# A graph-attention layer by leading columns: a new order of the drain, and tiles that start on round addresses

## The chip, the cores and the metric

The kernel runs on one core of a Trainium2 chip. The metric is device time in microseconds (us) of one execution; before the change it is 244.22 us, the median of 15 executions (243.28 to 246.55). Engines: TensorE (PE, with its weight loads PEld), VectorE (DVE), ScalarE (ACT), GpSimd (POOL) and SyncE (SP), which only issues transfers. Every engine works through its own queue in order; a wait at the head of a queue holds up all that stands behind it.

## The reference

`N = 4096` rows, `D = 512` features, 4 heads, all in float32:

```python
ht = (h @ W).reshape(N, N_HEADS, N_HIDDEN).transpose(1, 0, 2)
src = einsum('hnd,hd->hn', ht, a[:, :N_HIDDEN, 0])
dst = einsum('hnd,hd->hn', ht, a[:, N_HIDDEN:, 0])
e = leaky_relu(src[:, :, None] + dst[:, None, :], 0.01) + adj_mat[None]
att = softmax(e, axis=-1)
g = einsum('hij,hjd->hid', att, ht).mean(axis=0)
out = layernorm(x + g)          # over the 512 features, eps 1e-5
```

The adjacency matrix (4096 x 4096, 64 MB) holds values up to 1e9 that are added to the scores. Where the largest entry of a row lies far enough above the second, softmax puts all weight on that one column, and the row's result is `x[column] @ mean of the heads of W`.

## The kernel before, in words

`leading_rows` computes all rows in that way and tests that it was allowed; `general`, behind a branch, recomputes blocks in which a row failed the test. With these inputs no block is recomputed.

Rows are cut into 32 blocks (NB) of 128. With Q = 4, LATE = 28 and BEHIND = 24. Iteration `t` of the main loop works on several blocks at once:

- SP loads the adjacency rows of block t + 5 (`load_adj`, L113; 2 MB, 16 KB in each of 128 partitions; blocks 0 and 28 to 31 in four pieces of 4 KB per partition). Six buffers `adj_t` hold them. x comes into the big tile `hold` in groups of four blocks (`load_x`, L116); W lies in the places of blocks 16 to 31 of `hold` at first, so the x of blocks 24 to 31 is loaded only after the loop.
- VectorE takes the maxima of 64 segments of each row of block t (`segment_maxima`, L158), finds the leading segment (`find_segment`, L165 to L167), and GpSimd gathers that segment (`lead`, L171) by an indirect DMA.
- For block t - 2 VectorE finds the column within the segment (`find_column`, L193), GpSimd adds (L195) and gathers the rows of x (`y`, L181). Block 31 is searched in its whole row instead (`find_column_in_row`, L201, 4096 columns).
- For block t - 3 TensorE transposes y in four pieces (`turn`, L208), ScalarE copies the result to SBUF (`yt`, L210), and TensorE multiplies by the mean of the heads in four products over a quarter of the features each (`products`, L221). Blocks below BEHIND get x added on TensorE by a product with the identity (`residual`, L214).
- ScalarE does the layer norm's statistics with accumulating passes (`stats`, L243 and L245), the sum of squares of x for the test (`row_norm`, L228) and the final scaling (`finish`, L261); GpSimd makes the reciprocal root (`rstd`, L248 to L250). The results of blocks 24 to 27 are copied out of PSUM (`put_by`, L234) into a free adjacency buffer.

The order of every queue is the order of the program text. After the loop comes the drain, also written out by hand. It holds the loads of x for blocks 24 to 31, the 18 stores (L306, all on SP, each waiting for its data in the order of the program), the last two searches, the products of blocks 29 to 31, the addition of x to blocks 24 to 27 on VectorE (`add_x`, L237), the test in three parts (`bound`, L360 to L370, `test`, L376 to L382, `count`, L386, `report`, L390 to L393), and the normalisation: blocks 24 to 27 by `stats`, `rstd` or `rstd_late` (L254 to L257) and `finish`; blocks 28, 29 and 30 by `finish_last` (L294 to L303: add x, statistics and scaling on VectorE, only the root on ScalarE); block 31, whose products are in two halves of 256 columns (`products_of_half`, L270), by `finish_in_halves` (L279 to L286).

Where the tiles start, in bytes within a partition: `hold` at 17,312 (160 past a multiple of 256), the first `adj_t` at 96,992 (224 past one; all six alike), the first `y` at 204,032 (a multiple of 256), the first `lead` at 196,896 (32 past one). Tiles of the pools lie one behind the other, each rounded up to 32 bytes.

Of the kernel before, what the change touches and what calls it, by code (L numbers as in the profile page):

```python
# [9 lines left out]
F32 = mybir.dt.float32  # L10
# [3 lines left out]
OP = mybir.AluOpType  # L14
# [3 lines left out]
EPS = 1e-5  # L18
# [48 lines left out]
def leading_rows(ctx, tc, x, adj, W, a, out, ident, v, n_bad, any_bad):  # L67
# [17 lines left out]

    once = ctx.enter_context(tc.tile_pool(name="once", bufs=1))
    adj_pool = ctx.enter_context(tc.tile_pool(name="adj_pool", bufs=AHEAD + 1))
    small = ctx.enter_context(tc.tile_pool(name="small", bufs=5))
    rows = ctx.enter_context(tc.tile_pool(name="rows", bufs=2))
    psum = ctx.enter_context(tc.tile_pool(name="psum", bufs=4, space=bass.MemoryType.PSUM))  # L90
# [4 lines left out]
    out_rows = out.rearrange("(p nb) d -> p nb d", nb=NB)  # L95
    w_blocks = W.rearrange("(kb p) (h d) -> p kb h d", p=P, h=H)

    hold = once.tile([P, NB, D], F32, name="hold")
    w_at = NB - KB * H
    w_sum = once.tile([P, KB, D], F32, name="w_sum")  # L100
    a_rows = once.tile([2 * H, D], F32, name="a_rows")

    adj_t = {}

    def pieces(ib):
# [9 lines left out]
    def load_x(lo, n):  # L115
        nc.sync.dma_start(hold[:, ds(lo, n), :], x_rows[:, ds(lo, n), :])  # L116
# [46 lines left out]
    def find_segment(ib):  # L163
        seg = seg_of.pop(ib)
        nc.vector.max(out=top[:, ib, :], in_=seg)  # L165
        at = small.tile([P, 8], U32, name="at")
        nc.vector.max_index(at, top[:, ib, :], seg)  # L167
        row = small.tile([P, 1], U32, name="row")
        nc.gpsimd.tensor_tensor(row, at[:, 0:1], first[:, ib : ib + 1], op=OP.add)  # L169
        lead = small.tile([P, E], F32, name="lead", bufs=2 * Q + 1)  # L170
        nc.gpsimd.indirect_dma_start(  # L171
            out=lead, out_offset=None, in_=adj_segs,
            in_offset=bass.IndirectOffsetOnAxis(ap=row[:, :1], axis=0),
        )
        start = at_of[ib] = small.tile([P, 1], U32, name="start")
        nc.gpsimd.tensor_tensor(start, at[:, 0:1], width, op=OP.mult)
        lead_of[ib] = lead

    def gather_rows(ib, col):
        y = y_t[ib] = rows.tile([P, D], F32, name="y", bufs=4)  # L180
        nc.gpsimd.indirect_dma_start(  # L181
            out=y, out_offset=None, in_=x,
            in_offset=bass.IndirectOffsetOnAxis(ap=col[:, :1], axis=0),
        )

    def find_inner(ib):
        nc.vector.max(out=inner[:, ib, :], in_=lead_of[ib])

    def find_column(ib):
        if ib < BEHIND:  # L190
            find_inner(ib)
        within = small.tile([P, 8], U32, name="within")
        nc.vector.max_index(within, top[:, ib, :], lead_of[ib])  # L193
        col = small.tile([P, 1], U32, name="col")
        nc.gpsimd.tensor_tensor(col, at_of.pop(ib), within[:, 0:1], op=OP.add)  # L195
        gather_rows(ib, col)
# [19 lines left out]
    def products(ib, lo=0, hi=KB):  # L216
        start = ib not in o_ps
        if start:
            o_ps[ib] = psum.tile([P, D], F32, name="o")
        for kb in range(lo, hi):  # L220
            nc.tensor.matmul(  # L221
                o_ps[ib], yt_of[ib][:, kb, :], w_sum[:, kb, :],
                start=(start and kb == 0), stop=(kb == KB - 1),
            )
# [8 lines left out]
            o_ps["by"] = adj_pool.tile([P, N // D, D], F32, name="adj_t")  # L233
        nc.scalar.copy(o_ps["by"][:, ib - BEHIND, :], o_ps.pop(ib))  # L234

    def add_x(ib):
        nc.vector.tensor_add(hold[:, ib, :], hold[:, ib, :], o_ps["by"][:, ib - BEHIND, :])  # L237
        o_ps[ib] = hold[:, ib, :]

    def stats(ib):  # L240
# [6 lines left out]
    def rstd(i):  # L247
        nc.gpsimd.tensor_scalar(sd[:, i], sd[:, i], 1.0 / D, EPS, op0=OP.mult, op1=OP.add)  # L248
        nc.gpsimd.tensor_tensor(sd[:, i], sd[:, i], power[:, : i.stop - i.start], op=OP.pow)
        nc.gpsimd.tensor_mul(nm[:, i], nm[:, i], sd[:, i])  # L250

    def rstd_late(i):

        nc.vector.tensor_scalar(sd[:, i], sd[:, i], 1.0 / D, EPS, op0=OP.mult, op1=OP.add)  # L254
        nc.scalar.activation(sd[:, i], sd[:, i], AF.Sqrt)
        nc.vector.reciprocal(sd[:, i], sd[:, i])
        nc.vector.tensor_mul(nm[:, i], nm[:, i], sd[:, i])  # L257

    def finish(ib):
        i = slice(ib, ib + 1)  # L260
# [11 lines left out]
                start=False, stop=(kb == KB - 1),  # L272
            )

    def finish_in_halves(ib):
        halves = o_ps.pop(ib)
        st = small.tile([P, 2, nc.vector.BN_STATS_DIM], F32, name="st2", bufs=1)
        for k in range(2):
            nc.vector.bn_stats(st[:, k, :], halves[k])  # L279
        mv = small.tile([P, nc.vector.BN_AGGR_DIM], F32, name="mv", bufs=2)  # L280
        nc.vector.bn_aggr(mv, st)
        r = small.tile([P, 1], F32, name="r", bufs=2)
        nc.scalar.activation(r, mv[:, 1:2], AF.Sqrt, bias=eps)
        nc.vector.reciprocal(r, r)
        for k in range(2):
            nc.vector.tensor_scalar(  # L286
                hold[:, ib, ts(k, D // 2)], halves[k], mv[:, 0:1], r, op0=OP.subtract, op1=OP.mult
            )

    def finish_last(ib, residual):  # L290

        o = o_ps.pop(ib)
        if residual:
            nc.vector.tensor_add(hold[:, ib, :], o, hold[:, ib, :])  # L294
            o = hold[:, ib, :]
        st = small.tile([P, nc.vector.BN_STATS_DIM], F32, name="st", bufs=2)
        nc.vector.bn_stats(st, o)
        mv = small.tile([P, nc.vector.BN_AGGR_DIM], F32, name="mv", bufs=2)
        nc.vector.bn_aggr(mv, st)
        r = small.tile([P, 1], F32, name="r", bufs=2)  # L300
        nc.scalar.activation(r, mv[:, 1:2], AF.Sqrt, bias=eps)
        nc.vector.reciprocal(r, r)
        nc.vector.tensor_scalar(hold[:, ib, :], o, mv[:, 0:1], r, op0=OP.subtract, op1=OP.mult)  # L303

    def store(queue, lo, n):
        queue.dma_start(out_rows[:, ds(lo, n), :], hold[:, ds(lo, n), :])  # L306
# [93 lines left out]
    for t in range(NB):  # L400
        if t == NB // 2:
            tc.mark_branch_hint_location("general", engines=HINTED)
        if t in x_at:
            load_x(*x_at[t])
        load_adj(t + AHEAD)
        middle = 1 if t > LATE else 2
        segment_maxima(t, 0, middle)
        if t >= COLUMN:
            find_column(t - COLUMN)
        segment_maxima(t, middle, PIECES)  # L410
        pair = FINISH <= t < BEHIND + FINISH and t % 2 == 0
# [31 lines left out]
    for ib in range(BEHIND, NB, 2):  # L443
        load_x(ib, 2)
    for ib in range(0, BEHIND, 2):
        store(nc.sync, ib, 2)
    find_column(NB - 2)
    find_column_in_row(NB - 1)
    for ib in range(BEHIND, NB - 2):
        row_norm(ib)  # L450
    turn(NB - 3)
    for ib in range(NB - 2, NB):
        row_norm(ib)
    products(NB - 3, 0, KB - 1)
    finish_last(NB - 4, True)
    bound(0)
    turn(NB - 2)
    add_x(BEHIND)
    add_x(BEHIND + 1)
    products(NB - 3, KB - 1, KB)  # L460
    residual_in_halves(NB - 1)
    products(NB - 2, 0, 1)
    bound(1)
    products(NB - 2, 1, KB - 1)
    add_x(BEHIND + 2)
    add_x(BEHIND + 3)
    stats(BEHIND)
    stats(BEHIND + 1)
    rstd(slice(BEHIND, BEHIND + 2))
    for ib in range(BEHIND, NB):  # L470
        find_inner(ib)
    bound(2)
    test()
    pg = count()
    stats(BEHIND + 2)
    turn(NB - 1)
    finish_last(NB - 3, True)
    report(pg)
    finish(BEHIND)
    finish(BEHIND + 1)  # L480
    stats(BEHIND + 3)
    products(NB - 2, KB - 1, KB)
    products_of_half(NB - 1, 0)
    products_of_half(NB - 1, 1)
    rstd_late(slice(BEHIND + 2, LATE))
    finish_last(NB - 2, True)
    finish(BEHIND + 2)
    finish(BEHIND + 3)
    for ib, n in ((NB - 4, 1), (NB - 3, 1), (BEHIND, 2), (NB - 2, 1), (BEHIND + 2, 2)):
        store(nc.sync, ib, n)  # L490
    finish_in_halves(NB - 1)
    store(nc.sync, NB - 1, 1)


# [151 lines left out]
```

## Time and profile before

| | |
|---|---|
| median of 15 executions | 244.22 us |
| the profiled execution: its time, its span | 244.76 us, 243.2 us |
| TensorE busy | 193.8 us (80%) |
| VectorE busy | 189.2 us (78%) |
| ScalarE busy | 112.3 us (46%) |
| GpSimd busy | 96.4 us (40%) |
| bytes moved | 97.73 MB, 402 GB/s over the span |
| mean granted clock of TensorE | 0.972 |

The span runs from the first to the last instruction of the profiled execution; what lies around it (1.56 us here) is in its time too. A row in order of time gives start, duration, engine, line, operation and what it writes and reads, with a count where several were merged; in brackets stands how long the engine sat idle before it and what it waited for. A row of a group gives the count, the busy time in all and the mean of one in ns. A row of a stretch gives the busy time of each engine in it (TensorE, its weight loads, VectorE, ScalarE, GpSimd), the granted clock, the share of the transfer engines in use and GB/s.

### The profile page before, as it was taken

How to read it: one execution, taken by the hardware profiler on the slowest of the kernel's cores; microseconds unless marked ns; L12 is line 12 of the kernel's file. 1: busy time of each engine (PE TensorE's matmuls, PEld its weight loads, DVE VectorE, ACT ScalarE, POOL GpSimd, SP SyncE). 2: the span in 40 equal slices, each digit the busy share in tenths (PEclk: the TensorE clock that was granted, in tenths of full speed). 3: DMA queues.
4: the chain of work that ended last, by engine and by line, in shares of the span. 5: the costliest groups of instructions: out<-in, count | busy, mean ns of one | idle time of the engine just before them, and what ended most of it. 6: DMA issues, size and time to landing. Idle time of an engine off the chain costs nothing.

```text
span 243.2 us, 2510 instructions
## 1 busy us (share of the span) xinstructions
PE 193.8 (80%) x679; PEld 100.5 (41%) x679; DVE 189.2 (78%) x312; ACT 112.3 (46%) x270; POOL 96.4 (40%) x209
## 2 busy tenths in 40 slices
PE   0178839999999999999969779595979878777950
PEld 0034415655555555555324324242434433333530
DVE  2635785499679986999589969795998999899553
ACT  2012002155757575757646555352455841193961
POOL 1112322326425643655254636463456474441100
PEclk9999988999999999999999999998899999999995
DMA  6999999999999999999999999999999999999944
GB/s 247 441 410 420 424 438 410 420 434 412 422 423 419 410 438 410 424 413 438 415 422 416 435 419 414 425 420 420 420 426 392 407 408 406 408 415 416 398 166 175
DMA packets 14993, 97.73 MB, mean 402 GB/s; under 512 B 2296, under 2 KB 2296, under 8 KB 10240
## 3 DMA queue, kind: packets, MB, share of 16 engines
q1 hardware_dynamic: 11376, 88.09, 87.4%
q0 software_dynamic: 3584, 9.44, 9.8%
q8 instruction: 6, 0.10, 0.2%
q14 instruction: 11, 0.09, 0.1%
q10 hardware_dynamic: 16, 0.02, 0.0%
HBM read 89.15 MB, written 8.39 MB: 401 GB/s over the span
## 4 chain that ended last, share of the span: by engine, by line


## 5 line engine op out<-in xcount | busy, mean ns | idle before, releaser
L158 DVE TENSOR_REDUCE seg<-adj_t 128x32 f32<-128x2048 f32 (+1 forms) x74 | 146.3, 1987 | 38.3 <-DMA adj_t<-in_adj_dram 37.9
L221 PE MATMUL o<-w_sum,yt 128*128 128x512 f32 x248 | 114.8, 604 | 4.2 <-ACT yt L210 4.2
L221 PEld LDWEIGHTS o<-w_sum,yt 128*128 128x128 f32 x248 | 44.8, 191 | 56.9 <-issue 43.6
L210 ACT COPY yt<-tp 128x512 f32<-128x512 f32 x32 | 18.8, 587 | 50.8 <-PE tp L208 47.5
L171 POOL DMA_INDIRECT lead<-in_adj_dram,row x32 | 32.2, 1008 | 14.2 <-POOL row L169 14.2
L181 POOL DMA_INDIRECT y<-in_x_dram,col x32 | 30.8, 963 | 17.6 <-POOL col L195 15.1
L311 PE MATMUL o<-hold,ident 128*128 128x512 f32 x32 | 18.1, 718 | 18.4 <-DMA hold<-in_L_gnn_W_dram 18.4
L208 PE MATMUL tp<-ident,y 128*128 128x128 f32 x128 | 20.2, 281 | 14.4 <-DMA y<-in_x_dram,col 14.4
L208 PEld LDWEIGHTS tp<-ident,y 128*128 128x128 f32 x128 | 14.6, 143 | 27.3 <-issue 26.3
L214 PE MATMUL o<-hold,ident 128*128 128x512 f32 x48 | 25.5, 613 | 0.0
L195 POOL TENSOR_TENSOR col<-start,within 128x1 uint32<-128x1 uint32 x31 | 5.9, 190 | 47.7 <-DVE within L193 47.6
L329 ACT COPY wt<-tp 128x512 f32<-128x512 f32 x16 | 9.2, 588 | 31.5 <-PE tp L327 31.5
L169 POOL TENSOR_TENSOR row<-at,first 128x1 uint32<-128x1 uint32 x32 | 6.1, 190 | 41.4 <-DVE at L167 41.4
L228 ACT ACTIVATE sq<-hold 128x512 f32<-128x512 f32 x32 | 19.8, 619 | 0.0
L335 PEld LDWEIGHTS pv<-at_d,wt 128*128 128x128 f32 x128 | 16.3, 191 | 6.8 <-ACT wt L329 3.7
L311 PEld LDWEIGHTS o<-hold,ident 128*128 128x128 f32 x32 | 7.0, 229 | 27.2 <-POOL row L169 11.3
L312 ACT ACTIVATE w_sum<-o 128x512 f32<-128x512 f32 x4 | 2.4, 598 | 33.9 <-PE o L311 33.9
L261 ACT ACTIVATE hold<-o,nm,sd 128x512 f32<-128x512 f32 x24 | 17.3, 771 | 0.0
L245 ACT ACTIVATE sq<-o,nm 128x512 f32<-128x512 f32 x24 | 16.5, 688 | 0.8
L335 PE MATMUL pv<-at_d,wt 128*128 128x2 f32 x128 | 15.3, 244 | 0.6 <-ACT wt L329 0.6
L243 ACT ACTIVATE sq<-o 128x512 f32<-128x512 f32 x24 | 14.6, 607 | 0.0
L327 PEld LDWEIGHTS tp<-ident,hold 128*128 128x128 f32 x64 | 7.9, 142 | 6.9 <-issue 6.9
(87 smaller groups left out, 135.5 us busy)
## 6 DMA issues: line engine op xcount, KB each, us to landing
adj_t<-in_adj_dram SPq DMA_DIRECT2D x27, 2048.0 KB
adj_t<-in_adj_dram SPq DMA_DIRECT2D x20, 512.0 KB
out_dram<-hold SPq DMA_DIRECT2D x14, 512.0 KB
hold<-in_x_dram SPq DMA_DIRECT2D x6, 1024.0 KB
hold<-in_L_gnn_W_dram SPq DMA_DIRECT2D x4, 1024.0 KB
hold<-in_x_dram SPq DMA_DIRECT2D x4, 512.0 KB
out_dram<-hold SPq DMA_DIRECT2D x4, 256.0 KB
lead<-in_adj_dram,row POOLq DMA_INDIRECT x32, 6.0
```

Of the source, the lines that this page charges most:

```text
L158: nc.vector.tensor_reduce(seg_of[ib][:, ts(k, S // n)], adj_t[ib][:, ts(k, N // n)].rearrange("p (s e) -> p s e", e=E), axis=AX.X, op=OP.max,)
L171: nc.gpsimd.indirect_dma_start(out=lead, out_offset=None, in_=adj_segs, in_offset=bass.IndirectOffsetOnAxis(ap=row[:, :1], axis=0),)
L181: nc.gpsimd.indirect_dma_start(out=y, out_offset=None, in_=x, in_offset=bass.IndirectOffsetOnAxis(ap=col[:, :1], axis=0),)
L208: nc.tensor.transpose(tp[:, kb, :], y[:, ts(kb, P)], ident)
L210: nc.scalar.copy(yt, tp)
L214: nc.tensor.matmul(o_ps[ib], ident, hold[:, ib, :], start=True, stop=False)
L221: nc.tensor.matmul(o_ps[ib], yt_of[ib][:, kb, :], w_sum[:, kb, :], start=(start and kb == 0), stop=(kb == KB - 1),)
L228: nc.scalar.activation(sq, hold[:, ib, :], AF.Square, accum_out=xx[:, ib : ib + 1])
L245: nc.scalar.activation(sq, o, AF.Square, bias=nm[:, i], accum_out=sd[:, i])
L261: nc.scalar.activation(hold[:, ib, :], o_ps.pop(ib), AF.Identity, bias=nm[:, i], scale=sd[:, i])
L311: nc.tensor.matmul(o, ident, hold[:, w_at + kb * H + h, :], start=(h == 0), stop=(h == H - 1))
L335: nc.tensor.matmul(pv[:, kb, h : 2 * H : H], wt[:, k, :], at_d[:, k, h : 2 * H : H], start=(k == 0), stop=(k == KB - 1),)
```

## The change

The change rewrites the drain and shifts tiles in memory; what is computed stays the same.

In the last iteration of the loop the loads of x for blocks 24 to 31 are issued (in the order 24, 28, 26, 30, two blocks each), and block 24's x is added on GpSimd, ahead of the search for block 31's segment. Blocks 25 and 26 are added on GpSimd after the gathers of blocks 30 and 31. Block 27 is added on VectorE and gets its statistics there (`moments`) in place of ScalarE's. Blocks 28 and 29 get x by the identity product on TensorE, as the early blocks do. From block 25 on the last of a block's four products stands behind the transposes of the block after it. `finish_last` is split into `moments`, `factor` and `normalise`, whose calls are placed singly; `rstd_late` is gone. Block 31's statistics are taken one half at a time, and its second half is scaled on ScalarE. The first four blocks are stored with one transfer instead of two.

A tile of 96 bytes ahead of `hold`, one of 128 bytes behind `a_rows` and separate pools for `y` and `lead` move the starts: `hold` to 17,408, `adj_t` to 97,280, `y` to 195,584, `lead` to 203,776; all are multiples of 256, the first three of 512.

```diff
+    y_pool = ctx.enter_context(tc.tile_pool(name="y_pool", bufs=4))
+    lead_pool = ctx.enter_context(tc.tile_pool(name="lead_pool", bufs=2 * Q + 1))
...
+    once.tile([P, 24], F32, name="pad")
     hold = once.tile([P, NB, D], F32, name="hold")
...
+    once.tile([P, 32], F32, name="pad_end")
...
-    def add_x(ib):
-        nc.vector.tensor_add(hold[:, ib, :], hold[:, ib, :], o_ps["by"][:, ib - BEHIND, :])
+    def add_x(engine, ib):
+        engine.tensor_add(hold[:, ib, :], hold[:, ib, :], o_ps["by"][:, ib - BEHIND, :])
...
+    def moments(ib):
+        if ib < NB - 1:
+            st = small.tile([P, nc.vector.BN_STATS_DIM], F32, name="st", bufs=2)
+            nc.vector.bn_stats(st, o_ps[ib])
+        else:
+            st = halves_st
+        mv = mean_var[ib] = small.tile([P, nc.vector.BN_AGGR_DIM], F32, name="mv", bufs=3)
+        nc.vector.bn_aggr(mv, st)
+        r = rt[ib] = sd[:, ib : ib + 1]
+        nc.scalar.activation(r, mv[:, 1:2], AF.Sqrt, bias=eps)
+    def factor(ib, shift=False):
+        nc.vector.reciprocal(rt[ib], rt[ib])
+        if shift:
+            nc.vector.scalar_tensor_tensor(
+                nm[:, ib : ib + 1], mean_var[ib][:, 0:1], -1.0, rt[ib], op0=OP.mult, op1=OP.mult
+            )
+    def normalise(ib, o, columns=slice(0, D)):
+        nc.vector.tensor_scalar(
+            hold[:, ib, columns], o, mean_var[ib][:, 0:1], rt[ib], op0=OP.subtract, op1=OP.mult
+        )
+    def stats_of_half(ib, k):
+        nc.vector.bn_stats(halves_st[:, k, :], o_ps[ib][k])
     def finish_in_halves(ib):
+        halves, i = o_ps.pop(ib), slice(ib, ib + 1)
+        normalise(ib, halves[0], slice(0, D // 2))
+        nc.scalar.activation(hold[:, ib, D // 2 :], halves[1], AF.Identity, bias=nm[:, i], scale=sd[:, i])
...
+        if t == NB - 1:
+            for ib in (BEHIND, LATE, BEHIND + 2, LATE + 2):
+                load_x(ib, 2)
+            row_norm(BEHIND)
+            row_norm(BEHIND + 1)
+            add_x(nc.gpsimd, BEHIND)
         find_segment(t)
...
             turn(ib)
-            if ib < BEHIND:
+            if ib > BEHIND:
+                products(ib - 1, KB - 1, KB)
+            if ib < BEHIND or ib == LATE:
                 residual(ib)
...
-            products(ib)
+            products(ib, 0, KB if ib < BEHIND else KB - 1)
```

The drain after the change, in full:

```python
row_norm(BEHIND + 2); row_norm(BEHIND + 3); row_norm(LATE)
store(nc.sync, 0, Q)
for ib in range(Q, BEHIND, 2):
    store(nc.sync, ib, 2)
find_column(NB - 2)
add_x(nc.gpsimd, BEHIND + 1)
find_column_in_row(NB - 1)
add_x(nc.gpsimd, BEHIND + 2)
turn(NB - 3)
products(NB - 4, KB - 1, KB)
residual(NB - 3)
products(NB - 3)
for ib in range(LATE + 1, NB):
    row_norm(ib)
stats(BEHIND)
moments(LATE)
bound(0)
for ib in range(BEHIND, NB):
    find_inner(ib)
factor(LATE)
normalise(LATE, o_ps.pop(LATE))
turn(NB - 2)
residual_in_halves(NB - 1)
products(NB - 2, 0, 1)
bound(1)
add_x(nc.vector, LATE - 1)
stats(BEHIND + 1)
moments(LATE - 1)
products(NB - 2, 1, KB - 1)
rstd(slice(BEHIND, BEHIND + 2))
stats(BEHIND + 2)
bound(2)
test()
pg = count()
rstd(slice(BEHIND + 2, BEHIND + 3))
moments(NB - 3)
factor(LATE - 1, shift=True)
report(pg)
factor(NB - 3)
normalise(NB - 3, o_ps.pop(NB - 3))
turn(NB - 1)
finish(BEHIND); finish(BEHIND + 1)
products(NB - 2, KB - 1, KB)
products_of_half(NB - 1, 0); products_of_half(NB - 1, 1)
nc.vector.tensor_add(hold[:, NB - 2, :], o_ps[NB - 2], hold[:, NB - 2, :])
o_ps[NB - 2] = hold[:, NB - 2, :]
moments(NB - 2)
stats_of_half(NB - 1, 0)
factor(NB - 2)
normalise(NB - 2, o_ps.pop(NB - 2))
finish(BEHIND + 2); finish(BEHIND + 3)
stats_of_half(NB - 1, 1)
moments(NB - 1)
factor(NB - 1, shift=True)
finish_in_halves(NB - 1)
for ib, n in ((NB - 4, 1), (NB - 3, 1), (BEHIND, 2), (NB - 2, 1), (BEHIND + 2, 2)):
    store(nc.sync, ib, n)
store(nc.sync, NB - 1, 1)
```

More of the change, by code (lines that the diff above doesn't have):

```diff
@@ L169, in find_segment @@
         nc.gpsimd.tensor_tensor(row, at[:, 0:1], first[:, ib : ib + 1], op=OP.add)
-        lead = small.tile([P, E], F32, name="lead", bufs=2 * Q + 1)
+        lead = lead_pool.tile([P, E], F32, name="lead")
         nc.gpsimd.indirect_dma_start(
@@ L179, in gather_rows @@
     def gather_rows(ib, col):
-        y = y_t[ib] = rows.tile([P, D], F32, name="y", bufs=4)
+        y = y_t[ib] = y_pool.tile([P, D], F32, name="y")
         nc.gpsimd.indirect_dma_start(
@@ L250, in rstd @@
         nc.gpsimd.tensor_mul(nm[:, i], nm[:, i], sd[:, i])
[L252 to L257, printed above, removed]
     def finish(ib):
@@ L273, in products_of_half @@
             )
-    def finish_in_halves(ib):
[L276 to L303, printed above, removed]
+    mean_var, rt = {}, {}
@@ new lines, in normalise @@
+    def normalise(ib, o, columns=slice(0, D)):
+        nc.vector.tensor_scalar(
+            hold[:, ib, columns], o, mean_var[ib][:, 0:1], rt[ib], op0=OP.subtract, op1=OP.mult
+        )
+    halves_st = once.tile([P, 2, nc.vector.BN_STATS_DIM], F32, name="halves_st")
+    def stats_of_half(ib, k):
+        nc.vector.bn_stats(halves_st[:, k, :], o_ps[ib][k])
+    def finish_in_halves(ib):
+        halves, i = o_ps.pop(ib), slice(ib, ib + 1)
+        normalise(ib, halves[0], slice(0, D // 2))
+        nc.scalar.activation(hold[:, ib, D // 2 :], halves[1], AF.Identity, bias=nm[:, i], scale=sd[:, i])
@@ L441, in leading_rows @@
             finish(t - FINISH + 1)
-    for ib in range(BEHIND, NB, 2):
-        load_x(ib, 2)
-    for ib in range(0, BEHIND, 2):
+    row_norm(BEHIND + 2)
+    row_norm(BEHIND + 3)
+    row_norm(LATE)
+    store(nc.sync, 0, Q)
+    for ib in range(Q, BEHIND, 2):
         store(nc.sync, ib, 2)
     find_column(NB - 2)
+    add_x(nc.gpsimd, BEHIND + 1)
     find_column_in_row(NB - 1)
-    for ib in range(BEHIND, NB - 2):
-        row_norm(ib)
[L451 to L455, printed above, removed]
+    add_x(nc.gpsimd, BEHIND + 2)
+    turn(NB - 3)
+    products(NB - 4, KB - 1, KB)
+    residual(NB - 3)
+    products(NB - 3)
+    for ib in range(LATE + 1, NB):
+        row_norm(ib)
+    stats(BEHIND)
+    moments(LATE)
     bound(0)
+    for ib in range(BEHIND, NB):
+        find_inner(ib)
+    factor(LATE)
+    normalise(LATE, o_ps.pop(LATE))
     turn(NB - 2)
-    add_x(BEHIND)
-    add_x(BEHIND + 1)
-    products(NB - 3, KB - 1, KB)
     residual_in_halves(NB - 1)
@@ L463, in leading_rows @@
     bound(1)
+    add_x(nc.vector, LATE - 1)
+    stats(BEHIND + 1)
+    moments(LATE - 1)
     products(NB - 2, 1, KB - 1)
[L465 to L468, printed above, removed]
     rstd(slice(BEHIND, BEHIND + 2))
-    for ib in range(BEHIND, NB):
-        find_inner(ib)
+    stats(BEHIND + 2)
     bound(2)
@@ L474, in leading_rows @@
     pg = count()
-    stats(BEHIND + 2)
+    rstd(slice(BEHIND + 2, BEHIND + 3))
+    moments(NB - 3)
+    factor(LATE - 1, shift=True)
+    report(pg)
+    factor(NB - 3)
+    normalise(NB - 3, o_ps.pop(NB - 3))
     turn(NB - 1)
-    finish_last(NB - 3, True)
-    report(pg)
     finish(BEHIND)
     finish(BEHIND + 1)
-    stats(BEHIND + 3)
     products(NB - 2, KB - 1, KB)
@@ L484, in leading_rows @@
     products_of_half(NB - 1, 1)
-    rstd_late(slice(BEHIND + 2, LATE))
-    finish_last(NB - 2, True)
+    nc.vector.tensor_add(hold[:, NB - 2, :], o_ps[NB - 2], hold[:, NB - 2, :])
[4 more added lines that the diff above has]
+    normalise(NB - 2, o_ps.pop(NB - 2))
     finish(BEHIND + 2)
     finish(BEHIND + 3)
+    stats_of_half(NB - 1, 1)
+    moments(NB - 1)
+    factor(NB - 1, shift=True)
+    finish_in_halves(NB - 1)
     for ib, n in ((NB - 4, 1), (NB - 3, 1), (BEHIND, 2), (NB - 2, 1), (BEHIND + 2, 2)):
         store(nc.sync, ib, n)
-    finish_in_halves(NB - 1)
     store(nc.sync, NB - 1, 1)
```

## The prediction

> **What bounds the kernel now.** I read first the page's row of transferred bytes and the two queue rows, then busy time by stretch, then the drain in order of time.
>
> ```profile
> span 243.2 us, 2510 instructions
> GB/s 247 441 410 420 424 438 410 420 434 412 422 423 419 410 438 410 424 413 438 415 422 416 435 419 414 425 420 420 420 426 392 407 408 406 408 415 416 398 166 175
> q1 hardware_dynamic: 11376, 88.09, 87.4%
> q0 software_dynamic: 3584, 9.44, 9.8%
> ```
> ```profile
> 100.00:140.00 40.00, 35.72 (x123) 17.74 (x123) 35.04 (x58) 24.34 (x60) 19.93 (x43) 1.00 1.01 421
> 200.00:215.00 15.00, 11.90 (x36) 5.44 (x35) 13.62 (x27) 3.87 (x10) 6.05 (x13) 1.00 1.03 408
> 215.00:225.00 10.00, 7.56 (x25) 3.42 (x24) 9.53 (x17) 5.87 (x20) 3.05 (x5) 1.00 1.03 418
> 230.00:235.00 5.00, 4.19 (x18) 2.96 (x16) 2.23 (x11) 3.65 (x9) 0.00 (x0) 1.00 0.68 262
> 235.00:240.00 5.00, 0.00 (x0) 0.00 (x0) 3.58 (x10) 2.00 (x4) 0.00 (x0) 0.65 0.41 161
> ```
> The last columns of the second fence are granted clock, share of the transfer engines and GB/s. The transfers run full until about 230 us; in the last 13 us they are partly idle (0.68, 0.41), so there the compute sets the end and stores only follow it. VectorE's search falls behind the transfers only at the end: its last waits for adjacency data are
>
> ```profile
> 169.69 2.29 DVE L158 TENSOR_REDUCE seg<-adj_t 128x32 f32<-128x2048 f32 x1 [2.83 <-DMA adj_t<-in_adj_dram]
> 186.60 2.29 DVE L158 TENSOR_REDUCE seg<-adj_t 128x32 f32<-128x2048 f32 x1 [0.56 <-DMA adj_t<-in_adj_dram]
> ```
> From 186.6 it works without such a wait up to the search in the whole row (first row below), which releases the gather of block 31's rows of x. TensorE's part of the drain, and the two gathers it needs:
>
> ```profile
> 214.15 0.19 POOL L169 TENSOR_TENSOR row<-at,first 128x1 uint32<-128x1 uint32 x1 [2.34 <-DVE at L167]
> 214.76 4.42 DVE L201 FIND_INDEX8 col<-top,adj_t 128x8 uint32<-128x4096 f32 x1
> 216.43 0.96 POOL L181 DMA_INDIRECT y<-in_x_dram,col  x1 [0.27 <-POOL col L195]
> 217.48 0.60 PE L208 MATMUL tp<-ident,y 128*128 128x128 f32 x4
> 218.76 2.84 PE L221 MATMUL o<-w_sum,yt 128*128 128x512 f32 x6 [0.67 <-ACT yt L210]
> 219.94 0.95 POOL L181 DMA_INDIRECT y<-in_x_dram,col  x1 [2.54 <-issue]
> 223.63 0.63 PE L208 MATMUL tp<-ident,y 128*128 128x128 f32 x4 [1.40 <-DMA y<-in_x_dram,col]
> 224.09 1.02 PE L221 MATMUL o<-w_sum,yt 128*128 128x512 f32 x2
> 224.96 1.03 PE L266 MATMUL o<-hold,ident 128*128 128x256 f32 x4
> 226.77 0.38 PE L367 MATMUL px<-xg,ones 1*128 1x1 f32 x2
> 227.08 1.98 PE L221 MATMUL o<-w_sum,yt 128*128 128x512 f32 x4
> 228.99 0.22 PE L386 MATMUL px<-gap,ones 128*1 128x32 f32 x2
> 229.14 0.66 PE L208 MATMUL tp<-ident,y 128*128 128x128 f32 x4
> 229.63 1.02 PE L221 MATMUL o<-w_sum,yt 128*128 128x512 f32 x2
> 230.50 3.70 PE L270 MATMUL o<-w_sum,yt 128*128 128x256 f32 x16
> ```
> From 223.63 on TensorE is gapless: one start follows the other, and a product over one quarter of the features (two records) takes 0.87 us from start to start (224.09 to 224.96). Its last product ends at 230.50 + 3.70 = 234.20. What follows is VectorE and ScalarE alone:
>
> ```profile
> 233.51 0.17 DVE L254 TENSOR_SCALAR sd<-sd 128x2 f32<-128x2 f32 x1 [1.76 <-ACT sq L245]
> 234.23 0.69 DVE L294 TENSOR_TENSOR hold<-o,hold 128x512 f32<-128x512 f32 x1
> 234.96 0.69 DVE L297 BATCH_NORM_STATS2 st<-hold 128x6 f32<-128x512 f32 x1
> 236.10 1.50 ACT L261 ACTIVATE hold<-hold,nm,sd 128x512 f32<-128x512 f32 x2
> 236.43 0.55 DVE L303 TENSOR_SCALAR hold<-hold,mv,r 128x512 f32<-128x512 f32 x1
> 236.89 0.76 DVE L279 BATCH_NORM_STATS2 st<-o 128x6 f32<-128x256 f32 x2
> 237.68 0.21 DVE L281 BATCH_NORM_AGGREGATE mv<-st 128x2 f32<-128x12 f32 x1
> 237.92 0.29 ACT L283 ACTIVATE r<-mv,eps 128x1 f32<-128x1 f32 x1 [0.32 <-DVE mv L281]
> 238.25 0.17 DVE L284 RECIPROCAL r<-r 128x1 f32<-128x1 f32 x1 [0.36 <-ACT r L283]
> 238.45 1.00 DVE L286 TENSOR_SCALAR hold<-o,mv,r 128x256 f32<-128x256 f32 x2
> ```
> Compute ends at 239.45, that is 5.25 us after TensorE; 243.2 - 239.45 = 3.75 us more go into issuing and landing the last store. The 5.25 us hold work that was ready long before: VectorE stood still for 1.76 us in front of the statistics of blocks 26 and 27, then did block 30 (whose last product ended at 229.63 + 1.02), and only then block 31.
>
> **The change, part by part.** The sum is made against the profiled execution (span 243.2 in 244.76 us), which lies 0.54 above the median of 244.22; I subtract from the median.
>
> *TensorE.* Today block 29's last product stands behind block 30's transposes (224.09, 0.87 us on the path). Now it runs before they can start. Added are the identity products of blocks 28 and 29 (2 x 0.87). Each stands where TensorE waits today for ScalarE's copy of a transposed block: 28's before block 29's transposes, 29's in the 0.67 us gap ahead of 218.76. From 217.48: transposes 0.46 (as 223.63 to 224.09), block 28's last product 0.87, identity 0.87, four products 3.48, the small transpose 0.3 gives 223.4. Block 30's rows arrive for 223.63, so the cover is just enough: 0.2 us spare; gone, the identity products cost up to 1.74. From 223.63 the order is as today without the one product: TensorE ends at 234.20 - 0.87 = 233.33. Block 31's transposes then come at about 228.2; its gather is issued at 219.94, and with the 7.2 us that block 30's took (216.43 to 223.63) its rows are there at 227.1. The copy of its transpose now waits in ScalarE's queue behind the root for block 29, and that behind VectorE's test. The test feeds the matmul at 228.99 and follows that at 226.77; both come 0.87 sooner, so it is over at 227.6 to 228.1. Statistics, aggregate and root (0.7 + 0.2 + 0.3, rows below) bring the root to 228.8 to 229.3, the copy's 0.6 ends at 229.4 to 229.9, and the product that covers it at 228.2 + 0.46 + 0.87 = 229.5.
>
> ```profile
> L210 ACT COPY yt<-tp 128x512 f32<-128x512 f32 x32 | 18.8, 587 | 50.8 <-PE tp L208 47.5
> ```
> So 0 to 0.4 us; I take the lower end, since what stands just ahead of the matmul at 228.99 today is TensorE's own products (227.08 + 1.98), not the test.
>
> *VectorE's end.* Of the additions of x, 24 to 26 leave VectorE, 28's and 29's go to TensorE; the statistics of 27 move to it, early, between the parts of the bound. Block 30's addition, statistics and scaling (0.7 + 0.7 + 0.2, then 0.2 + 0.55) now fit under block 31's products (3.70). After TensorE's end remain: statistics of one half 0.4, aggregate 0.21, root 0.29, reciprocal 0.17, the shift 0.2, one half scaled 0.5 on VectorE and the other beside it on ScalarE, with some 0.15 between them: 1.9 us in place of 5.25. ScalarE's own finish of blocks 26 and 27 (1.50) starts when block 30's root is done, near 232.2, and is over at 233.7, before the last root at 234.0. So compute ends at 235.2, and with the same 3.75 the span at 239.0: **4.2 us less**. Stores are in no one's way: the transfers are idle half the time here.
>
> *The sums on GpSimd.* A 128x512 addition on GpSimd is in no row. Nearest are
>
> ```profile
> masks.py:199 POOL TENSOR_SCALAR_AFFINE_SELECT ident<-ident 128x128 f32<-128x128 f32 x1 | 0.3, 293 | 0.1
> L237 DVE TENSOR_TENSOR hold<-hold,adj_t 128x512 f32<-128x512 f32 x4 | 2.6, 676 | 0.0
> ```
> From below VectorE's 0.68; from above four times GpSimd's 128 columns for each of two operands, 2.3 us. I take 1.2. Block 24's stands ahead of the index of block 31's segment and, behind that, of block 30's gather; GpSimd is idle there for 2.34 us. Block 25's stands ahead of block 31's gather, idle 2.54. Block 26's follows it, with only the reciprocal roots behind. So nothing, at either end of the price. [...]
>
> *The loads* of x move ahead of no other transfer: all adjacency loads are issued by then. Two ScalarE sums of squares go ahead of block 28's copy and have their data by then, as today's later ones never wait.
>
> *The starts of tiles.* The lists of the kernel's tiles put hold 160 bytes and the adjacency buffers 224 bytes past a multiple of 256; padding brings both to 0. y already starts on such a multiple. No row prices this. If the queues share one price per byte and one per packet, the two queue rows (share x 243.2 us x 16 engines: 3401 and 381 us) give 37.7 ns per KB and 7.1 ns per packet, so queue 1, whose tiles start off a multiple, and queue 0, which is mostly y, lie on one line: nothing to gain. Were all of queue 1's packet time due to its starts, 11376 x 7.1 / 16 = 5.0 us would go. Loads in 4 KB pieces ran at 408 GB/s, stores in such pieces at 418: if that difference is the starts, it is 2.4% of some 26 us and a quarter of that on 150 us of 16 KB rows, together 1.5 us. A loss, from all tiles starting alike, I bound by the same 1.5. I take 0.8, half of the nearest row's. A gain reaches the search: with 0.56 and 2.83 us of waits VectorE follows the data.
>
> Sum: 244.22 - 4.2 - 0.8 = **239.2 us**.
>
> **The rivals.** *Starts cost bytes.* If each transfer pays for the bytes from the multiple of 256 below its start, 16 KB rows carry 224 / 16384 = 1.4%, 4 KB pieces 5.5%, x and W in 8 KB 2%. Up to the search that is 56.6 MB at 421 GB/s x 1.35%, 10.5 MB x 5.2%, 10.5 MB x 1.9%, 2 MB x 3.8%: 1.8 + 1.3 + 0.5 + 0.2 = 3.8 us, and 236.2 us in all. For it: 421 against 408 is near the 4% it asks. Against: 7.1 ns for every packet asks the same, and stores at 418 lie too high for it. [...]
>
> *TensorE is too full.* The two identity products aren't covered: + 1.74, so 241.0 us, or 241.8 without gain from starts. For it: 0.2 us of cover. Against: today's gaps of 0.67 and 1.40.
>
> *GpSimd holds the gathers: slower.* With P for one addition, block 30's gather slips by P - 2.34, and block 31's by 2P - 4.9 (216.43 + 0.96 + 2P - 2.34 against 219.94). Block 31's rows have 1.1 us of slack. At P = 4.9 us the slip is 4.9 and eats 1.1 and nearly all of the gain; from there it is slower, at P = 6 by about 2: 246 us. For it: GpSimd's power on two columns takes 0.72 us,
>
> ```profile
> L249 POOL TENSOR_TENSOR sd<-sd,power 128x2 f32<-128x2 f32 x13 | 9.4, 724 | 1.1
> ```
> so its prices aren't smooth. Against: its products of two columns take 0.2, and 128 columns 0.29.
>
> **How the numbers follow.** Forecast 0.58 (238.2 to 240.6), starts cost bytes 0.18 (236 to 238.2), TensorE too full 0.13 (240.6 to 242.5), GpSimd 0.11 (of which 0.07 slower, 0.04 no change). Range 236.6 to 242.2: it leaves out the outer part of both sides. A measurement tells 0.5% (1.2 us) from no change: faster 0.88, same 0.05, slower 0.07.
>
> **What would show it.** TensorE's last product ending near 233.3 less what the search gains; 1.9 us from there to the end of compute; no wait of 1.76 us in VectorE's tail; GpSimd's additions of 1 to 2 us inside idle time, with unchanged distance from search to gather; loads in 4 KB pieces above 408 GB/s if starts matter. The forecast is wrong if block 31's transposes start after 229, if ScalarE's copy of them waits for VectorE, or if the last store waits for stores ahead of it.

## The result, and the profile after

The changed kernel takes 237.54 us in the median (236.96 to 239.12, 9 executions) against 244.43 us of the kernel before in the same comparison: a ratio of 0.9724, 95% interval 0.9695 to 0.9752. The forecast was 239.2 us; the gain is 6.7 us by the ratio and 6.9 by the medians, where 5.0 were forecast. The profiled execution took 237.1 us with a span of 235.5 us.

The page of the changed kernel, its rows of bytes and queues:

```profile
span 235.5 us, 2519 instructions
GB/s 241 432 427 419 443 420 433 424 432 413 443 419 429 420 431 437 431 418 429 436 429 431 426 431 423 427 423 431 426 424 414 418 417 419 419 425 414 420 380 227
q1 hardware_dynamic: 11232, 88.09, 88.8%
q0 software_dynamic: 3584, 9.44, 10.1%
```

The same bytes go through in a shorter span. Busy time by stretch of the changed kernel (last columns: granted clock, share of the transfer engines, GB/s):

```profile
100.00:140.00 40.00, 37.26 (x128) 18.46 (x126) 35.18 (x59) 25.74 (x62) 19.64 (x41) 1.00 1.01 429
200.00:215.00 15.00, 12.66 (x38) 5.46 (x37) 13.11 (x22) 6.33 (x16) 9.31 (x16) 1.00 1.03 420
225.00:230.00 5.00, 5.00 (x24) 3.65 (x22) 4.11 (x14) 4.00 (x7) 0.74 (x3) 1.00 0.93 368
230.00:235.50 5.50, 0.06 (x1) 0.00 (x0) 1.42 (x5) 0.86 (x2) 0.00 (x0) 0.98 0.54 217
```

Two things differ from before. The loads run at 429 GB/s where they ran at 421 (100 to 140 us, long before the drain begins), and at 420 where they ran at 408 (200 to 215 us). And the stretch with idle transfers at the end has shrunk from some 13 us to about 8. The drain of the changed kernel in order of time:

```profile
208.44 0.63 ACT L233 ACTIVATE sq<-hold 128x512 f32<-128x512 f32 x1 [2.97 <-DMA hold<-in_x_dram]
209.24 1.27 POOL L242 TENSOR_TENSOR hold<-hold,adj_t 128x512 f32<-128x512 f32 x1 [0.76 <-ACT sq L233]
210.13 0.58 ACT L215 COPY yt<-tp 128x512 f32<-128x512 f32 x1 [0.36 <-PE tp L213]
210.28 0.22 DVE L172 FIND_INDEX8 at<-top,seg 128x8 uint32<-128x64 f32 x1
210.58 0.19 POOL L174 TENSOR_TENSOR row<-at,first 128x1 uint32<-128x1 uint32 x1
212.42 4.42 DVE L206 FIND_INDEX8 col<-top,adj_t 128x8 uint32<-128x4096 f32 x1
213.19 0.96 POOL L186 DMA_INDIRECT y<-in_x_dram,col  x1 [0.54 <-POOL col L200]
214.58 0.63 PE L213 MATMUL tp<-ident,y 128*128 128x128 f32 x4 [0.26 <-DMA y<-in_x_dram,col]
217.60 0.96 POOL L186 DMA_INDIRECT y<-in_x_dram,col  x1 [2.15 <-issue]
220.31 0.60 PE L213 MATMUL tp<-ident,y 128*128 128x128 f32 x4
225.01 0.66 PE L213 MATMUL tp<-ident,y 128*128 128x128 f32 x4
226.37 3.70 PE L268 MATMUL o<-w_sum,yt 128*128 128x256 f32 x16
230.10 0.43 DVE L302 BATCH_NORM_STATS2 halves_st<-o 128x6 f32<-128x256 f32 x1 [0.65 <-PE o L268]
231.41 0.54 DVE L295 TENSOR_SCALAR hold<-o,mv,sd 128x256 f32<-128x256 f32 x1
231.53 0.56 ACT L308 ACTIVATE hold<-o,nm,sd 128x256 f32<-128x256 f32 x1 [0.42 <-DVE nm L290]
```

The search ends at 212.42 + 4.42 = 216.84 us (before: 219.18), TensorE at 226.37 + 3.70 = 230.07 (before: 234.20), compute at 231.53 + 0.56 = 232.09 (before: 239.45). VectorE now waits for TensorE's last product (0.65 ahead of 230.10); before, that product was done at 234.20 and its statistics began only at 236.89. From the end of compute to the end of the span it is 3.41 us (before: 3.75). So 2.3 us of the gain were there when the search ended, 1.8 more when TensorE ended, 3.2 more when compute ended and 0.3 more at the end of the span: 7.7 us between these two executions, of which the one before lay 0.5 above its median and the one after 0.4 below.

### The profile page after: what moved, and what is told of

Its sections match the earlier page's. It is cut to its first block, busy times and chain, and to the rows that moved or that the text cites. A ratio compares the mean times of both kernels' runs of the same rounds, so it can differ in the third digit from the quotient of the medians.

```text
span 235.5 us, 2519 instructions
## 1 busy us (share of the span) xinstructions
PE 198.8 (84%) x683; PEld 102.6 (44%) x683; DVE 186.6 (79%) x308; ACT 111.6 (47%) x267; POOL 100.9 (43%) x215
## 4 chain that ended last, share of the span: by engine, by line
PE 44%; DMA 20%; issue 17%; POOL 14%; ACT 2%; DVE 0%; SPq 0%; POOLq 0%
PE o L226 23%; DMA hold<-in_L_gnn_W_dram 11%; DMA y<-in_x_dram,col 6%; PE o L219 5%; PE pv L340 5%; POOL y L186 4%; POOL lead L176 4%; PE tp L213 4%; PE o L316 3%; DMA adj_t<-in_adj_dram 3%; PE tp L332 2%; POOL sd L254 2%; PE o L268 2%; POOL start L181 1%; POOL col L200 1%
## 5 line engine op out<-in xcount | busy, mean ns | idle before, releaser
L316 PE MATMUL o<-hold,ident 128*128 128x512 f32 x32 | 22.0, 852 | 15.9 <-DMA hold<-in_L_gnn_W_dram 15.9
L219 PE MATMUL o<-hold,ident 128*128 128x512 f32 x52 | 27.5, 611 | 0.0
L316 PEld LDWEIGHTS o<-hold,ident 128*128 128x128 f32 x32 | 8.4, 274 | 26.9 <-POOL row L174 11.8
```

What stands on the lines that cost most here:

```text
L219: nc.tensor.matmul(o_ps[ib], ident, hold[:, ib, :], start=True, stop=False)
L316: nc.tensor.matmul(o, ident, hold[:, w_at + kb * H + h, :], start=(h == 0), stop=(h == H - 1))
```

## The experiments

Each was timed against the kernel before on the chip it ran on (ratio with 95% interval). Differences in us are those of the ratios, times 244.

**The two parts apart.** First the new drain with the old starts; hold lies again 160 and the adjacency buffers 224 bytes past a multiple of 256, lead 32 past one, y on one.

```diff
-    once.tile([P, 24], F32, name="pad")
-    once.tile([P, 32], F32, name="pad_end")
+    once.tile([P, 48], F32, name="pad_end")
-    y_pool = ...; lead_pool = ...
+    # y again in the pool rows, lead in the pool small
...
+    small.tile([P, 24], F32, name="pad_small", bufs=1)
```

> The new drain alone, with the old starts (hold 160, adjacency buffers 224 past a multiple of 256). Theory: the two parts are apart. The search ended 2.3 us sooner after the change (219.18 to 216.84 us) because the loads ran at 429 in place of 421 GB/s, and the drain behind the search took 4.6 to 5 us less. So about 239.7 us here, with loads at 421 GB/s. Rival: the drain's new order brings the search forward too and the starts do nothing: 237.5 us, as with the whole change.

Measured: ratio 0.9865 (0.9847 to 0.9883), 3.3 us less; 240.72 us. Then the starts alone, in the old drain:

```diff
+    once.tile([P, 24], F32, name="pad")
     hold = once.tile([P, NB, D], F32, name="hold")
...
+    once.tile([P, 48], F32, name="pad_end")
+    # y and lead in pools of their own
```

> The old drain with the new starts alone. Theory: loads at 429 GB/s, search 2.3 us sooner, the old drain's 20.3 us behind it unchanged: about 242.1 us. Rival: starts do nothing, 244.4 us. Second rival (each transfer pays for the bytes from the multiple of 256 below its start): 3.8 us less, 240.6 us.

Measured: ratio 0.9897 (0.9864 to 0.9930), 2.5 us less; 241.66 us. Its loads run at 428 GB/s between 60 and 140 us, those of the drain alone at 422, as before the change (422). Its search ends at 216.35 us, and TensorE and VectorE follow in the old order; compute ends 20.6 us behind the search, before the change 20.3. All three rivals fall: the starts are worth 2.5 us by themselves, not 0 and not 3.8, and the new drain brings no search forward (it ends at 219.48 with the old starts). But the theory's 239.7 us for the drain alone was 1.0 us short.

Together the parts give 5.8 us, the whole change 6.7. The times alone don't show that anything is missing: their intervals are 0.4, 0.8 and 0.7 us to either side. The trace of the drain alone does show a loss, first by stretch:

```profile
230.00:235.00 5.00, 2.81 (x14) 2.13 (x12) 3.41 (x11) 3.02 (x6) 0.00 (x0) 1.00 0.98 385
235.00:239.20 4.20, 0.00 (x0) 0.00 (x0) 0.00 (x0) 0.00 (x0) 0.00 (x0) 0.58 0.32 123
```

and in order of time (the same kernel, drain alone):

```profile
212.43 1.27 POOL L239 TENSOR_TENSOR hold<-hold,adj_t 128x512 f32<-128x512 f32 x1 [1.26 <-ACT sq L230]
212.96 0.22 DVE L169 FIND_INDEX8 at<-top,seg 128x8 uint32<-128x64 f32 x1
213.65 0.19 POOL L171 TENSOR_TENSOR row<-at,first 128x1 uint32<-128x1 uint32 x1
229.12 3.70 PE L265 MATMUL o<-w_sum,yt 128*128 128x256 f32 x16
234.28 0.56 ACT L305 ACTIVATE hold<-o,nm,sd 128x256 f32<-128x256 f32 x1 [0.43 <-DVE nm L287]
```

Compute ends at 234.84 us, but the span at 239.2: 4.36 us later, against 3.41 with the new starts. The transfer engines are still in use to 0.98 from 230 to 235 us, so here the last store does wait for stores ahead of it: from the start of its first packet to the end of its last it takes 1.9 us, in the changed kernel 1.0 and in the kernel before 0.9. With the slower transfers (410 GB/s from 200 to 215 us, 420 in the changed kernel) the quicker compute runs into them. That difference, 0.95 us, is about the 0.9 us that the parts lack; that it is the same 0.9 us is likely but not shown.

**How round a start must be.** In the changed kernel all four tiles start on multiples of 512, lead too (203,776 is 398 times 512). In four kernels they (hold, adjacency buffers, y, lead) were moved on together by changing one number:

```diff
-    once.tile([P, 24], F32, name="pad")
+    once.tile([P, 32], F32, name="pad")     # 32 bytes on; 40: 64 bytes; 56: 128 bytes; 88: 256 bytes
```

> The whole change with every tile moved on by 32 bytes. The starts of before are 32 past a multiple of 64. Theory that a start needs a multiple of 64: the whole gain of the starts is gone, 239.8 us, loads at 421 GB/s. Theory of a price per byte below the start: 32 bytes, half of the 64-byte case, 238.0 us.

> The whole change with every tile moved on by 64 bytes (hold, adjacency buffers, y and lead all 64 past a multiple of 256). Theory that a start needs only a multiple of 64: as the whole change, 237.5 us, loads at 429 GB/s. Theory of 256 with a price per byte below the start: 64 of 16384 and of 4096 bytes, 0.4% and 1.6%, about 0.9 us more, 238.4. Theory that any start off 256 costs the same: 239.8 us.

> The whole change with every tile 128 bytes past a multiple of 512. Loads ran at 429 GB/s with starts on 512, at 419 with all starts 64 past, at 418 with all 32 past. Theory that a multiple of 128 is enough: 429 GB/s and 237.3 us. Theory that 256 or 512 is needed: 419 to 421 GB/s and 240 to 242.5 us.

> The whole change with every tile 256 bytes past a multiple of 512. Theory that 256 is enough: 429 GB/s, 237.3 us. Theory that 512 is needed: 419 to 421 GB/s, 240 to 242.5 us.

**Whose start.** Then single tiles: hold alone 32 bytes past; the adjacency buffers alone 64; lead alone 64; y and lead 64.

```diff
 # hold alone
-    once.tile([P, 24], F32, name="pad")
+    once.tile([P, 32], F32, name="pad")
-    once.tile([P, 32], F32, name="pad_end")
+    once.tile([P, 24], F32, name="pad_end")
 # adjacency buffers alone
-    once.tile([P, 32], F32, name="pad_end")
+    once.tile([P, 48], F32, name="pad_end")
+    y_pool.tile([P, 48], F32, name="pad_y", bufs=1)
 # y and lead
+    y_pool.tile([P, 16], F32, name="pad_y", bufs=1)
 # lead alone
+    lead_pool.tile([P, 16], F32, name="pad_lead", bufs=1)
```

> The whole change with hold alone 32 bytes past; adjacency buffers, y and lead on multiples of 512 or 256. Theory that each load pays for its own start: x and W are 10.5 of 80 MB and the stores leave from hold, so most of the gain stays, about 238.0 us, 16 KB rows at 427 to 429 GB/s. Rival that one badly placed stream slows all: 240 us.

> The whole change with the gathered tiles y and lead alone 64 bytes past. In the kernel before, y lay on a multiple of 256; with all tiles moved the time came out 2 us worse than with the old starts. Theory that y's start is what made that difference: 1 to 2 us more than the whole change, 238.5 to 239.5 us. Rival that y's 8.4 MB pay only in proportion to the loads' 80 MB: 0.3 us more, 237.7 us.

> The whole change with the adjacency buffers alone 64 bytes past a multiple of 256; hold, y and lead on such multiples. Moving hold alone cost nothing, moving y and lead alone took the loads from 429 to 422 GB/s and 2 us. Theory that the adjacency loads pay for their own start: 421 to 425 GB/s and 239 to 240 us. Rival that only the gathered tiles matter: 429 GB/s, 237.2 us.

> The whole change with lead alone 64 bytes past a multiple of 256 (rows of 256 bytes, which then reach over two such pieces). Theory that lead's start did the harm when y and lead were moved: 422 GB/s, 239.2 us. Rival that y's did: 429 GB/s, 237.2 us.

All of them together. GB/s are those of the stretch from 60 to 140 us (mostly adjacency rows in 16 KB) and of 200 to 215 us (4 KB pieces: the last of the adjacency, x, the first stores); the last columns are mean times of one transfer packet in the trace: adjacency rows in 16 KB, adjacency pieces of blocks 28 to 31 in 4 KB, pairs of gathered rows y.

| starts past a multiple of 256 | ratio (95%) | us | GB/s | 16 KB, ns | 4 KB, ns | y, ns |
|---|---|---|---|---|---|---|
| new drain: hold 160, adj 224, lead 32, y 0 | 0.9865 (0.9847 to 0.9883) | 240.72 | 422, 410 | 620.7 | 164.1 | 161.7 |
| all 0 (multiple of 512): the change | 0.9724 (0.9695 to 0.9752) | 237.54 | 429, 420 | 611.8 | 159.1 | 160.1 |
| all 0 (256 past a multiple of 512) | 0.9720 (0.9674 to 0.9765) | 237.16 | 428, 420 | 612.1 | 159.1 | 159.9 |
| all 128 | 0.9929 (0.9904 to 0.9953) | 242.41 | 419, 402 | 624.5 | 166.0 | 163.1 |
| all 64 | 0.9938 (0.9921 to 0.9955) | 242.55 | 419, 402 | 624.3 | 165.8 | 163.3 |
| all 32 | 0.9951 (0.9935 to 0.9966) | 242.91 | 418, 404 | 625.5 | 165.4 | 163.0 |
| hold 32, others 0 | 0.9715 (0.9670 to 0.9760) | 237.11 | 428, 420 | 611.9 | 159.3 | 159.9 |
| lead 64, others 0 | 0.9729 (0.9695 to 0.9763) | 237.52 | 427, 419 | 613.1 | 159.2 | 160.1 |
| adj 64, others 0 | 0.9740 (0.9706 to 0.9774) | 237.84 | 427, 416 | 612.8 | 161.4 | 160.6 |
| y and lead 64, others 0 | 0.9803 (0.9758 to 0.9849) | 239.25 | 422, 419 | 617.8 | 159.9 | 160.5 |

The rows of two of these, the stretch from 60 to 140 us; first with all starts 128 bytes past, then 256:

```profile
60.00:140.00 80.00, 75.52 (x291) 41.51 (x290) 67.58 (x106) 47.41 (x114) 38.79 (x83) 0.98 1.01 419
```
```profile
60.00:140.00 80.00, 75.50 (x294) 41.40 (x292) 68.72 (x109) 48.63 (x116) 38.97 (x83) 1.00 1.01 428
```

What follows. A multiple of 256 is enough (428 GB/s, 237.16 us) and 128 is not (419 GB/s, 242.41 us); expectations that 64 or 128 would do fell. With all starts 64 or 32 past, every theory on record was too low (at most 239.8 us; measured 242.55 and 242.91): these kernels are 2 us worse than the one with the old starts, in which y stood on a multiple of 256. Off such a multiple the price hardly depends on the distance: 32, 64 and 128 bytes cost the same 5 us within 0.5, where a price per byte would go as 1 to 2 to 4. hold alone pays nothing that shows (428 GB/s, 237.11 us): x and W are loaded into it and all stores leave from it, and the packets of 8 KB, nearly all of them loads of x and W, took 309.9 ns with hold 32 bytes past against 310.5 in the changed kernel (319.8 with all starts 64 past). Adjacency buffers alone or lead alone cost no more than the intervals can tell; the 4 KB packets of the former are 2.3 ns longer. y and lead together cost 2 us, and the packets that get longer are not y's own (160.5 against 160.1 ns) but the adjacency rows' (617.8 against 611.8). y alone was not moved.

The single prices (0, 0.1, 0.4 and 1.9 us by the ratios, each within 1.3 or less) don't add up to the 5 us of all, nor do those of hold, adjacency buffers and lead to the 2.5 of the starts of before. The time isn't the cleanest measure here, since the drain can add to it (below); but the 16 KB packets say the same: 0.1 ns more with hold off, 1.0 with the adjacency buffers, 6.0 with y and lead, 12.5 with all at 64. Which pairs make each other worse, and why, stays open.

The kernels with everything moved also lose in the drain. All starts 64 bytes past, in order of time:

```profile
213.12 0.63 ACT L233 ACTIVATE sq<-hold 128x512 f32<-128x512 f32 x1 [4.02 <-DMA hold<-in_x_dram]
213.84 0.22 DVE L172 FIND_INDEX8 at<-top,seg 128x8 uint32<-128x64 f32 x1
213.92 1.27 POOL L242 TENSOR_TENSOR hold<-hold,adj_t 128x512 f32<-128x512 f32 x1 [1.88 <-ACT sq L233]
214.57 1.13 PE L219 MATMUL o<-hold,ident 128*128 128x512 f32 x2 [0.91 <-DMA hold<-in_x_dram]
215.15 0.18 POOL L174 TENSOR_TENSOR row<-at,first 128x1 uint32<-128x1 uint32 x1
215.29 4.42 DVE L206 FIND_INDEX8 col<-top,adj_t 128x8 uint32<-128x4096 f32 x1
217.19 0.96 POOL L186 DMA_INDIRECT y<-in_x_dram,col  x1 [0.27 <-POOL col L200]
```

x of block 24 comes later, so GpSimd's addition starts only at 213.92 and holds the index for block 31's segment (its input is there at 214.06) until 215.15, 1.09 us late; with all starts 32 and 128 past it is 0.83 and 0.29 us late, in the changed kernel 0.08. Block 30's gather, behind it, is issued at 217.19, 2.52 us ahead of the search's end (219.71) in place of 3.65 in the changed kernel. TensorE's identity product for block 28 waits for its x too (0.91 us at 214.57).

**The place of GpSimd's first addition.** A second addition of 512 columns was put behind it, into a tile that nothing reads.

```diff
             add_x(nc.gpsimd, BEHIND)
+            nc.gpsimd.tensor_add(once.tile([P, D], F32, name="spare"), o_ps[BEHIND], o_ps[BEHIND])
         find_segment(t)
```

> The whole change with a second addition of 512 columns on GpSimd (into a tile that nothing reads) between block 24's and the index of block 31's segment. The changed kernel's block-24 addition ran from 209.24 to 210.51 us and the index came at 210.58, so the place is full. Theory: the second one, 1.27 us, pushes the index, the gathers of block 30's rows and TensorE behind it by some 1.2 us: 238.4 to 238.8 us. Theory of the prediction (2.34 us idle at this place): nothing, 237.4 us.

Measured: ratio 0.9740 (0.9701 to 0.9778), 237.73 us. The intervals of this and of the changed kernel overlap, so the time doesn't tell the theories apart. The trace does:

```profile
208.63 1.27 POOL L242 TENSOR_TENSOR hold<-hold,adj_t 128x512 f32<-128x512 f32 x1 [0.63 <-ACT sq L233]
209.81 0.22 DVE L172 FIND_INDEX8 at<-top,seg 128x8 uint32<-128x64 f32 x1
209.99 1.04 POOL L425 TENSOR_TENSOR spare<-hold 128x512 f32<-128x512 f32 x1
210.98 0.19 POOL L174 TENSOR_TENSOR row<-at,first 128x1 uint32<-128x1 uint32 x1
213.04 0.96 POOL L186 DMA_INDIRECT y<-in_x_dram,col  x1 [0.27 <-POOL col L200]
```

The index's input is there at 210.03, and the index comes at 210.98, directly behind the second addition: 0.95 us late, against 0.08 in the changed kernel. TensorE ends at 231.12 us, later than in the changed kernel and the four others that have this drain and adjacency buffers and y on round starts (229.58 to 230.44). So the place is full, as expected. The delay is 0.9 us and not 1.27, because this addition, with one operand twice, took only 1.04.

**One identity product less.** Block 29's x is added on VectorE again.

```diff
-    residual(NB - 3)
-    products(NB - 3)
+    products(NB - 3, 0, KB - 1)
...
-    turn(NB - 2)
     residual_in_halves(NB - 1)
+    turn(NB - 2)
+    products(NB - 3, KB - 1, KB)
...
+    nc.vector.tensor_add(hold[:, NB - 3, :], o_ps[NB - 3], hold[:, NB - 3, :])
+    o_ps[NB - 3] = hold[:, NB - 3, :]
     products(NB - 2, 1, KB - 1)
```

> The whole change with x of block 29 added on VectorE again, in its wait for the bound's second matmul, and with TensorE's identity product for block 31 ahead of block 30's transposes, block 29's last product behind them. Theory: TensorE is gapless from block 29's transposes (214.58) to its end (230.07), so 0.87 us less there comes out as 0.2 to 0.9 us, the rest being taken by the wait for block 31's rows: 236.6 to 237.2 us. Rival: block 30's rows aren't there any sooner than today (220.3), nothing gained, 237.3 us.

Measured: ratio 0.9710 (0.9676 to 0.9743), 237.07 us: not to be told from the changed kernel. The trace goes with the rival:

```profile
212.43 0.96 POOL L186 DMA_INDIRECT y<-in_x_dram,col  x1 [0.27 <-POOL col L200]
220.33 0.63 PE L213 MATMUL tp<-ident,y 128*128 128x128 f32 x4 [1.00 <-DMA y<-in_x_dram,col]
226.41 3.70 PE L268 MATMUL o<-w_sum,yt 128*128 128x256 f32 x16
```

TensorE is through 0.87 us sooner and then waits 1.00 us for block 30's rows. They came at 220.33, no sooner than TensorE used them in the changed kernel (220.31), though their gather was issued 0.76 us sooner (212.43 against 213.19). So in this execution the identity product would have been free. In the changed kernel TensorE doesn't wait there, so its trace doesn't tell when the rows could be used: their last packet ended at 219.00, and where TensorE did wait for rows in that kernel it started 0.65 to 1.20 us behind the last packet. By that estimate the rows could be used 0.1 to 0.7 us before TensorE came to them, and the product cost it as much.

No experiment gave a version that is measurably faster than the changed kernel. The traces show one likely reason. Compute ends at 232.09 us in the changed kernel, at 231.74 with all starts moved by 256 bytes and at 231.60 with hold alone moved, but the spans end at 235.5, 235.6 and 235.4. There the last store's packets take 1.0, 1.5 and 1.4 us; compute that ends a little sooner meets the stores ahead of it.

## Why the prediction was right, and where a step of it was off

The outcome lay inside the range, but below the band of the forecast (238.2 to 240.6), in the band that the prediction gave to the rival that starts cost bytes (236 to 238.2). That rival's law is not what happened: compute in the drain went as forecast, and the starts brought three times the 0.8 us put down for them. Step by step:

- *TensorE ends at 233.33 us, without what the starts bring.* Right: 232.82 in the drain alone, 0.5 us sooner. The identity products are covered as forecast (in the changed kernel block 29's transposes waited 0.26 us for their rows, then TensorE had no gap), but for an estimated 0.1 to 0.7 us of block 29's (last experiment); TensorE was not too full.
- *The copy behind the root of block 29 costs 0 to 0.4 us, taken as nothing.* Right: transposes at 225.01, products of block 31 at 226.37, 1.36 us later, as in the kernel before (229.14 and 230.50).
- *1.9 us from TensorE's end to the end of compute.* Right: 2.02 both in the drain alone (232.82 to 234.84) and in the changed kernel (230.07 to 232.09).
- *The same 3.75 us after that; stores in no one's way.* Wrong for the drain alone: 4.36 us, where the last store takes 1.9 us in place of 0.9. So the drain by itself gave 3.3 us and not 4.2. In the whole change it is 3.41, 3.86 with all starts moved by 256 bytes. Of the 3.75, 2.0 us lay behind the last packet; with the new drain it is 1.5 to 1.6 in every kernel, and what shortened it stays open. The prediction took the idle transfers of the old drain as given, although the drain was to end 4 us sooner with the same bytes to store. The prediction named this among what would make it wrong.
- *GpSimd's addition at 1.2 us.* Right: 1.27 (block 24's, at 209.24 us in the changed kernel).
- *Its 2.34 us of idle cover.* Wrong in kind: the addition can't start when GpSimd falls idle. It waits for ScalarE's sum of squares of the same x, which waits for the load (2.97 us at 208.44). I had taken that data to be there, because the later sums of today never wait; they stand some 6 us later. In the changed kernel the addition ends just as the index's input arrives (210.51 and 210.50), so nothing was lost; in the drain alone the index came 0.47 us late (input at 213.18, index at 213.65), and with all starts 32 or 64 past 0.83 and 1.09.
- *0.8 us for the starts.* This is the term that was mis-sized: 2.5 us by themselves (1.7 to 3.3 by the interval). The step that failed is the line through the two queue rows, "nothing to gain": two rows fit any two prices, so their agreement said nothing about a third. The better lead was the one that I halved: loads at 408 GB/s against stores at 418, which gave 1.5.
- *The rival that starts cost bytes, 3.8 us.* Its law was a supposition that no row of the kernel before showed, and the runs refute it: 32, 64 and 128 bytes past cost the same 5 us within 0.5, and the starts of before cost 2.5 us. Its boundary of 256 bytes does show, for the tiles that transfers write (428 GB/s with all starts 256 past a multiple of 512, 419 with all 128 past); a price for the bytes below the start doesn't. Nor is it a price of each packet that starts off the multiple: with the adjacency buffers alone 64 bytes past, nine in ten of the 16 KB packets still took at most 613 ns, against 611 on round starts.
- *A gain in the loads reaches the search.* Right: the search ends 2.3 us sooner in the changed kernel and 2.8 in the one with the starts alone.

Of the 6.7 us, the runs put 3.3 on the drain and 2.5 on the starts. The remaining 0.9 is within the intervals; the traces suggest that it belongs to both, as with the faster loads the new drain's last store waits less. The drain by itself fell 0.9 us short of its 4.2, and the starts brought 1.7 more than their 0.8; that the two errors partly cancel in the sum is luck.

## What to carry to other kernels

In this kernel it paid to put the tiles that transfers write on multiples of 256 bytes within the partition, gathered tiles as well: with all of them off, the loads were about 2% slower (418 to 419 GB/s against 429), and a careless 64 bytes took back three quarters of the change's gain (242.55 us against 237.54). So look at the addresses after each change of a small tile ahead of such tiles. Where work moves into an engine's idle time, look up when its inputs arrive, not only when the engine is free. And where compute is to end sooner, ask whether the stores can follow.

## What the runs showed of the hardware that was not expected

- When all destinations in SBUF start off a multiple of 256 bytes, packets become longer and uneven. On round starts the adjacency packets of 16 KB take 611.8 ns in the mean, and nine in ten take 611; with all starts 128 past half take 618 or more, one in ten 638 or more and one in a hundred 686. The highest mean was 625.5 (32 past); 4 KB packets took 159.1 against up to 166.0.
- The price doesn't grow with the distance from the multiple (418 to 419 GB/s at 32, 64 and 128 bytes), and multiples of 256 and of 512 are alike (428 and 429).
- It is paid by other transfers too: with only the gathered tiles y and lead off, the adjacency loads fell from 429 to 422 GB/s, while the gathers' own packets took 160.5 ns in place of 160.1. Moving hold alone changed nothing that shows (428 GB/s).
- The price isn't a sum over tiles: 5 us and 12.5 ns per 16 KB packet with all at 64, at most 1.9 us and 6.0 ns with any one group off.
